# Experts' gate and up products in two halves, and scatters through views that do not overlap

## The chip, the cores and the metric

The kernel runs on one core of a Trainium2 chip. The time is the device time of one execution, in microseconds (us). The engines of the core run side by side and wait for each other through semaphores: TensorE (PE) multiplies and transposes, VectorE (DVE) and ScalarE (ACT) work element by element, GpSimd (POOL) does the same and issues the indirect scatters, and SyncE (SP) issues the ordinary DMAs.

## The reference

The input `x` has 8 sequences of 64 rows of 512 numbers, so 512 rows in all. Each context has 1601 rows of 512 numbers. All numbers are fp32. Three blocks follow one another, each added to `x`:

```
x = x + cross_attention(layernorm(x), ctx)       # one head of 512, softmax over 1601 rows
x = x + attention(layernorm(x))                  # 16 heads of 32, sigmoid instead of softmax
x = x + experts(layernorm(x))                    # 8 experts, each row goes to one
```

In the last block a row's expert is the largest of 8 gate products. The row, times the sigmoid of that largest product, goes through its expert: `g = xs @ w_gate.T`, `u = xs @ w_up.T` (512 to 256 each), then `(u * silu(g)) @ w_down.T` back to 512.

## The kernel before, in words

The 512 rows are four tiles of 128 (`i` or `p` from 0 to 3), two sequences each. A main loop over the tiles does the cross-attention of tile `p`, with the steps of the second block for tiles `p - 1` and `p - 2` between its products. Behind the loop stands an ending: the second block's steps for tiles 2 and 3, and the experts.

The steps are small functions with a name and a number, and `do(...)` calls them in the order in which they are written. PE's order is exactly this order, for a manual schedule is open on PE from the start; in the ending SP's order is written out too, and POOL's inside `routed`. The orders of DVE, ACT and, elsewhere, POOL are planned by the compiler from the dependences and its own costs. PE takes its instructions in order: one that waits holds up all behind it.

Steps of the second block for tile `i`, with the PE work that the trace shows for each:

- `turn`: four transposes of the normalized rows (`t_xh`), copied to `xhT` and `xvT` by DVE and ACT.
- `unit_q`, `unit_k`: a projection of four products, one for each chunk of 128 of the contraction (`p_q`, `p_k`; the trace counts two matmul instructions for each fp32 product), then a normalization by ACT and DVE.
- `gates`: POOL and DVE only. `values`: a projection (`p_v`), scaled by DVE.
- `split`: transposes of q and k (`t_q`, `t_k`). `align`: 64 small matmul instructions (`al`, L490), sigmoid by ACT into `res`.
- `sums`: 64 small matmul instructions (`co`, L508), scaled by DVE. `back`: transposes (`t_c`), copied by ACT into `cT`. `output`: a projection (`p_o`), added to `x` by DVE.
- `face`: transposes of the result (`t_x`). `gated`: the gate products (`pl`, L621, 8 columns wide) and a chain of tiny DVE instructions.
- `routed`: counts of rows for each expert (`pr`, `pf`), a slot for each row, and two indirect scatters by POOL into DRAM: the scaled rows into `xd` (L676), the rows with their index into `rd` (L699). A slot is a row of `xd` and `rd`; no two rows of `x` get the same.

Every row of `xd` belongs to one expert: parts of 32 rows, so that a tile of 128 slots holds 32 rows of each of four experts. Six such tiles (`k` from 0 to 5) are computed; even ones belong to experts 0 to 3, odd ones to experts 4 to 7. A later branch for the case that an expert gets more than 96 rows is not entered with these inputs. The steps of a tile:

- `fetch(part)`: SP loads tiles `2*part` and `2*part + 1` of `xd` and `rd` (L868). It waits for all scatters before it: `fetch(0)` stands behind those of `x` tiles 0 and 1, `fetch(1)` behind that of tile 2, `fetch(2)` behind that of tile 3.
- `flip(k)`: four transposes (`t_xe`), copied by ACT to `xeT`.
- `up(k)`: the gate and up products (`gu`, L879): for each of four chunks of the contraction, four experts side by side in the array, so 16 products, or 32 matmul instructions in the trace. Then ACT's sigmoid and two DVE products make `h`.
- `over(k)`: two transposes of `h` (`ht`, L893), copied by DVE to `hT`.
- `down(k)`: 8 products (`y`, L903, 16 instructions); DVE adds the rows of `rd` (L908), and POOL scatters the 128 rows into the result (L909). Slots that no row has taken carry an index that is out of bounds and are left out.

The ending of before, from the last steps of tile 2 on:

```
fetch(0)
do((turn, 2), (unit_q, 2), (at_turn, 3), (unit_k, 2), (at_out, 3), (norm, 3), (gates, 2))
do((values, 2), (split, 2), (turn, 3), (flip, 0), (up, 0), (align, 2), (unit_q, 3))
do((over, 0), (sums, 2), (unit_k, 3), (flip, 1), (back, 2), (down, 0), (gates, 3))
do((output, 2), (split, 3), (values, 3), (face, 2), (align, 3), (gated, 2), (sums, 3))
do((routed, 2))
```

PSUM has eight banks, which all products share (`bank`). The large row buffers are 22 of one size (`row`). Between instructions that touch the same DRAM tensor the framework sets a wait where it can't tell that their rows differ; the rows of an indirect scatter are known only at run time, so two scatters into one tensor wait for one another, by landing.

Of the kernel before, what the change touches and what calls it, by code (L numbers as in the profile page):

```python
# [8 lines left out]

# [10 lines left out]
NT = B * S // P  # L20
DC = D // P
# [4 lines left out]
PARTS = 3  # L26
# [9 lines left out]
def perceiver_kernel(ctx: ExitStack, tc: tile.TileContext, out: bass.AP, t: dict):  # L36
# [16 lines left out]
    def row(name):  # L53
        return rowp.tile([P, D], F32, tag="row", name=name)
# [4 lines left out]
    def bank(name):  # L59
        return banks.tile([P, D], F32, tag="bank", name=name)  # L60
# [4 lines left out]
    def tiny(n, tag, name):  # L65
        return small.tile([P, n], F32, tag=tag, name=name)
# [171 lines left out]
    with tc.manual_schedule(engines={mybir.EngineType.DVE, mybir.EngineType.Activation}):  # L238
# [19 lines left out]
        for i0 in (0, 2):  # L258
            cols = slice(i0 * P, (i0 + 2) * P)
            for ec in range(DC):  # L260
                ps = bank(f"qp{i0}_{ec}")
                for dc in range(DC):
                    nc.tensor.matmul(  # L263
                        ps[:, : 2 * P], lhsT=wq[:, dc, ec * P : (ec + 1) * P],
                        rhs=xnT[:, dc, cols], start=(dc == 0), stop=(dc == DC - 1),
# [265 lines left out]
    ffw = {}  # L531
# [10 lines left out]
    def load_experts():  # L542

        gu, dn = {}, {}
        gu[0] = load_gate_up(0, slab("wgu0"))
        gu[1] = load_gate_up(1, one.tile([P, DC, D], F32, tag="R", name="wgu1"))
        for e in range(2, E):
            if e - 2 < 5:
                dn[e - 2] = load_down(
                    e - 2, blkp.tile([P, IC, D], F32, tag="blk", name=f"wd{e - 2}")  # L550
                )
            gu[e] = load_gate_up(e, slab(f"wgu{e}"))
        return gu, dn
# [14 lines left out]
    xd = tc.dram_tile([E * ROWS, D], F32, name="xd")  # L568
    rd = tc.dram_tile([E * ROWS, D + 4], F32, name="rd")

    def blank_rows():
        blank = blkp.tile([P, D + 4], F32, tag="blk", name="blank")
        nc.gpsimd.memset(blank[:, :D], 0.0)
        nc.gpsimd.memset(blank[:, D:].bitcast(I32), 1 << 20)
        for r in range(0, E * CAP, P):
            nc.gpsimd.dma_start(out=xd[r : r + P, :], in_=blank[:, :D])
            nc.gpsimd.dma_start(out=rd[r : r + P, :], in_=blank)
# [63 lines left out]
    def route(i, mean, rs, begin):  # L641

        ps = bank(f"pr{i}")
        pr = ps[:, :E]
        if i > 0:
            nc.tensor.matmul(pr, lhsT=ones, rhs=runs[-1], start=True, stop=False)
        nc.tensor.matmul(pr, lhsT=before, rhs=oh[:, i, :], start=(i == 0), stop=True)
        if i > 0:
            nrun = const.tile([P, E], F32, tag=f"run{i}", name=f"run{i}")
            nc.gpsimd.tensor_tensor(nrun, runs[-1], oh[:, i, :], ALU.add)  # L650
            runs.append(nrun)
        else:
            runs.append(oh[:, i, :])
        at = tiny(E, "at", f"at{i}")
        nc.vector.tensor_tensor(at, pr, oh[:, i, :], ALU.mult)
        place = tiny(1, "place", f"place{i}")
        nc.vector.tensor_reduce(place, at, AX.X, ALU.add)
        slot_i = const.tile([P, 1], I32, tag=f"slot{i}", name=f"sloti{i}")
        if i < NT - 1:

            part = small.tile([P, 1], I32, tag="part", name=f"part{i}")
            nc.vector.tensor_copy(part, place)
            nc.vector.tensor_scalar(part, part, 0x7FE0, None, ALU.bitwise_and)
            at1 = tiny(1, "at1", f"at1_{i}")
            nc.vector.scalar_tensor_tensor(at1, part, E - 1.0, place, ALU.mult, ALU.add)
            nc.vector.tensor_scalar(slot_i, at1, begin, None, ALU.add)
        else:

            past = tiny(1, "at1", f"past{i}")
            nc.vector.tensor_scalar(past, place, CAP - 0.5, 4.0 * E * ROWS, ALU.is_ge, ALU.mult)  # L670
            nc.vector.scalar_tensor_tensor(slot_i, place, begin, past, ALU.add, ALU.add)
        by = tiny(1, "by", f"by{i}")
        nc.vector.tensor_tensor(by, rw[:, i : i + 1], rs, ALU.mult)
        xr = row(f"xr{i}")
        nc.vector.tensor_scalar(xr, xs[i], mean, by, ALU.subtract, ALU.mult)
        nc.gpsimd.indirect_dma_start(  # L676
            out=xd[:, :], out_offset=bass.IndirectOffsetOnAxis(ap=slot_i, axis=0),
            in_=xr, in_offset=None, bounds_check=E * ROWS - 1, oob_is_err=False,
        )
        return slot_i  # L680
# [16 lines left out]

    def send_rows(i, xb, slot_i):
        nc.gpsimd.indirect_dma_start(  # L699
            out=rd[:, :], out_offset=bass.IndirectOffsetOnAxis(ap=slot_i, axis=0),  # L700
            in_=xb, in_offset=None, bounds_check=E * ROWS - 1, oob_is_err=False,
        )

# [66 lines left out]
    def routed(i):  # L770
        xb = keep_rows(i)
        with tc.manual_schedule(engines={mybir.EngineType.Pool}):
            slot = route(i, *tile_of[i]["spread"])
            send_rows(i, xb, slot)
        if 0 < i < NT - 1:
            raised(i)
# [8 lines left out]
    def do(*steps):  # L785
        for f, i in steps:
            f(i)
# [15 lines left out]
    for p in range(NT):  # L803
        i = p - 2
# [27 lines left out]
        if p == 1:  # L832
            blank_rows()
# [21 lines left out]
    gu, dn = load_experts()  # L855
    NR = 2 * PARTS

    def columns(k):
        return [(4 * (k % 2) + j, slice(j * PART, (j + 1) * PART)) for j in range(4)]

    xes, xbs, xTs, hs = {}, {}, {}, {}

    def fetch(part):

        for src, dst in ((xd, xes), (rd, xbs)):
            for k in (2 * part, 2 * part + 1):
                dst[k] = rowp.tile([P, src.shape[-1]], F32, tag="row", name=f"in{k}_{src.shape[-1]}")
                nc.sync.dma_start(out=dst[k], in_=src[k * P : (k + 1) * P, :])  # L868
# [2 lines left out]
        xTs[k] = row4(f"xeT{k}")  # L871
        nc.scalar.copy(xTs[k], transposed(xes.pop(k), f"xe{k}"))  # L872

    def up(k):
        xT = xTs.pop(k)
        ps = bank(f"gu{k}")
        for dc in range(DC):
            for e, c in columns(k):
                nc.tensor.matmul(  # L879
                    ps[c, :], lhsT=xT[:, dc, c], rhs=ffw[e][0][:, dc, :],  # L880
                    start=(dc == 0), stop=(dc == DC - 1),
                )
        h = rowp.tile([P, FI], F32, tag="row", name=f"h{k}")
        nc.scalar.activation(h, ps[:, :FI], AF.Sigmoid)  # L884
        nc.vector.tensor_tensor(h, ps[:, :FI], h, ALU.mult)  # L885
        nc.vector.tensor_tensor(h, ps[:, FI:], h, ALU.mult)
        hs[k] = h
# [10 lines left out]
    def down(k):  # L898
        hT = hs.pop(k)
        y = bank(f"y{k}")  # L900
        for ic in range(IC):
            for e, c in columns(k):
                nc.tensor.matmul(  # L903
                    y[c, :], lhsT=hT[:, ic, c], rhs=ffw[e][1][:, ic, :],
                    start=(ic == 0), stop=(ic == IC - 1),
                )
        xb = xbs.pop(k)
        nc.vector.tensor_tensor(xb[:, :D], y, xb[:, :D], ALU.add)  # L908
        nc.gpsimd.indirect_dma_start(  # L909
            out=out[:, :],  # L910
            out_offset=bass.IndirectOffsetOnAxis(ap=xb[:, D : D + 1].bitcast(I32), axis=0),
            in_=xb[:, :D], in_offset=None, bounds_check=B * S - 1, oob_is_err=False,
        )
# [3 lines left out]
    fetch(0)  # L917
    load_experts_late(gu, dn)
    do((turn, 2), (unit_q, 2), (at_turn, 3), (unit_k, 2), (at_out, 3), (norm, 3), (gates, 2))
    do((values, 2), (split, 2), (turn, 3), (flip, 0), (up, 0), (align, 2), (unit_q, 3))  # L920
    do((over, 0), (sums, 2), (unit_k, 3), (flip, 1), (back, 2), (down, 0), (gates, 3))
    do((output, 2), (split, 3), (values, 3), (face, 2), (align, 3), (gated, 2), (sums, 3))
    do((routed, 2))
    fetch(1)
    do((up, 1), (back, 3), (over, 1), (output, 3), (down, 1), (face, 3), (flip, 2))
    do((gated, 3), (up, 2), (routed, 3))
    fetch(2)

    ps = bank("pc")
# [2 lines left out]
    nc.vector.tensor_reduce(most, ps[:, :E], AX.X, ALU.max)  # L932
    nc.vector.tensor_scalar(flag, most, CAP + 0.5, None, ALU.is_ge)

    do((over, 2), (flip, 3), (up, 3), (down, 2), (over, 3), (down, 3))
    do((flip, 4), (up, 4), (flip, 5), (over, 4), (up, 5), (down, 4), (over, 5), (down, 5))
    spill = nc.values_load(flag[0:1, 0:1], min_val=0, max_val=1)  # L937
    last.close()
    order.close()
# [3 lines left out]
    with tc.If(spill != 0), ExitStack() as ph:  # L943
# [16 lines left out]
        for e in range(E):  # L960
# [11 lines left out]
                wb, lhsT=ones, rhs=dg.rearrange("p i q -> p (i q)"), start=True, stop=True  # L972
# [6 lines left out]
            for ic in range(IC):  # L979
                pgu = []  # L980
                for k in range(2):
                    ps = ps_g.tile([P, B * S], F32, tag="gu", name=f"dgu{e}_{ic}_{k}")
                    for dc in range(DC):
                        c0 = k * FI + ic * P
                        nc.tensor.matmul(
                            ps, lhsT=wgu[:, dc, c0 : c0 + P], rhs=xsT[:, dc, :],
# [70 lines left out]
```

## Time and profile before

| what | value |
|---|---|
| three runs | 328.46, 331.7 and 332.65 us; median 331.7 |
| the profiled execution's own time | 333.91 us |
| its span, from the first to the last instruction | 332.2 us |
| mean granted TensorE clock | 0.95 |
| first instruction that the new order moves (`p_v` of tile 2 starts) | 232.38 us |
| last product (`y` of tile 5) ends | 324.26 us |
| last scatter is issued | 327.36 us |

The times of all views count from the start of the span. A group in the timeline has its start, its length, engine, line, operation, the tiles that it writes and reads, its shape and its count; in brackets stands how long the engine stood idle before it, and who released it. The windows view has for each stretch the busy time of PE, weight loads (PEld), DVE, ACT and POOL with their instructions, and then the granted clock, the DMA share and GB/s.

### The profile page before, as it was taken

How to read it: one execution, taken by the hardware profiler on the slowest of the kernel's cores; microseconds unless marked ns; L12 is line 12 of the kernel's file. 1: busy time of each engine (PE TensorE's matmuls, PEld its weight loads, DVE VectorE, ACT ScalarE, POOL GpSimd, SP SyncE). 2: the span in 40 equal slices, each digit the busy share in tenths (PEclk: the TensorE clock that was granted, in tenths of full speed). 3: DMA queues.
4: the chain of work that ended last, by engine and by line, in shares of the span. 5: the costliest groups of instructions: out<-in, count | busy, mean ns of one | idle time of the engine just before them, and what ended most of it. 6: DMA issues, size and time to landing. Idle time of an engine off the chain costs nothing. (4 is left out here: it accounts for less than half of the span.)

```text
span 332.2 us, 6425 instructions
## 1 busy us (share of the span) xinstructions
PE 298.7 (90%) x2652; PEld 157.5 (47%) x2652; DVE 161.9 (49%) x416; ACT 92.0 (28%) x192; POOL 60.7 (18%) x93
## 2 busy tenths in 40 slices
PE   5999699999999899998999999999699999889790
PEld 4776365643553245644434654434356464342220
DVE  5215477234751677655586845324614743452120
ACT  3133104330055020366331435314342240120100
POOL 4003630500161005001023000220400412031111
PEclk9799699999999999999999999999979985997996
DMA  8999800179893980000893028699601002305101
GB/s 275 426 418 310 346 6 2 37 275 417 316 353 110 386 325 6 4 0 8 314 372 132 2 84 299 224 310 357 248 2 65 29 2 67 125 28 174 54 7 35
DMA packets 19712, 57.71 MB, mean 174 GB/s; under 512 B 2210, under 2 KB 10450, under 8 KB 15712
## 3 DMA queue, kind: packets, MB, share of 16 engines
q1 hardware_dynamic: 16992, 50.37, 42.0%
q0 software_dynamic: 2400, 6.89, 5.6%
q8 instruction: 23, 0.38, 0.5%
q14 instruction: 9, 0.07, 0.1%
q10 hardware_dynamic: 288, 0.00, 0.0%
HBM read 50.94 MB, written 6.84 MB: 174 GB/s over the span
## 5 line engine op out<-in xcount | busy, mean ns | idle before, releaser
L221 DVE STREAM_TRANSPOSE T<-cx 128x512 f32<-128x512 f32 x96 | 61.8, 681 | 36.5 <-DMA cx<-in_ctx_dram 25.1
L326 PE MATMUL sc<-T,R 32*64 32x416 f32 (+2 forms) x1024 | 51.9, 524 | 2.8 <-DVE qb L291 2.7
L382 PE MATMUL ac<-cx,pt 128*64 128x512 f32 x192 | 43.8, 598 | 1.8 <-ACT pt L372 1.8
L326 PEld LDWEIGHTS sc<-T,R 32*64 32x64 f32 x1024 | 28.6, 138 | 21.8 <-issue 8.3
L879 PE MATMUL gu<-wgu,xeT 128*32 128x512 f32 x192 | 28.1, 732 | 4.8 <-ACT xeT L872 4.8
L382 PEld LDWEIGHTS ac<-cx,pt 128*64 128x64 f32 x192 | 12.7, 136 | 24.4 <-issue 21.2
L263 PE MATMUL qp<-xnT,w_xWq 128*128 128x256 f32 x64 | 15.9, 412 | 2.5 <-DMA w_xWq<-in_xWq_dram 1.7
L879 PEld LDWEIGHTS gu<-wgu,xeT 128*32 128x32 f32 x192 | 8.3, 130 | 19.8 <-issue 14.3
L457 POOL TENSOR_TENSOR gm_k<-qn_k,c_gk 128x512 f32<-128x512 f32 x4 | 5.1, 1272 | 67.2 <-DVE qn_k L452 67.2
L174 PE MATMUL p_q<-w_aWq,xhT 128*128 128x512 f32 x32 | 14.8, 605 | 2.5 <-DVE xhT L428 2.5
L885 DVE TENSOR_TENSOR h<-gu,h 128x256 f32<-128x256 f32 x6 | 2.5, 424 | 28.9 <-ACT h L884 28.9
L299 POOL COPY q<-qk 128x512 f32<-128x512 f32 x16 | 9.1, 615 | 40.8 <-ACT qk L284 40.8
L420 POOL TENSOR_TENSOR x<-x,c_bo 128x512 f32<-128x512 f32 x4 | 5.1, 1268 | 60.4 <-DVE xh L419 60.4
L263 PEld LDWEIGHTS qp<-xnT,w_xWq 128*128 128x128 f32 x64 | 13.1, 208 | 4.9 <-ACT rs_a L246 1.9
L174 PE MATMUL p_o<-w_aWo,cT 128*128 128x512 f32 x32 | 14.7, 602 | 0.7 <-ACT cT L524 0.7
L174 PE MATMUL p_po<-w_xWv,acT 128*128 128x512 f32 x32 | 14.5, 595 | 0.7 <-ACT acT L394 0.7
L174 PE MATMUL p_qk<-w_xWkT,qpT 128*128 128x512 f32 x32 | 14.7, 601 | 0.0
L174 PE MATMUL p_k<-w_aWk,xhT 128*128 128x512 f32 x32 | 14.5, 595 | 0.0
L174 PE MATMUL p_v<-w_aWv,xvT 128*128 128x512 f32 x32 | 14.4, 592 | 0.0
L372 ACT COPY pt<-pp 128x512 f32<-128x512 f32 (+1 forms) x16 | 7.8, 525 | 23.2 <-PE pp L370 23.1
L903 PE MATMUL y<-wd,hT 128*32 128x512 f32 x96 | 11.5, 596 | 1.6 <-DVE hT L895 1.6
L337 DVE TENSOR_REDUCE mx<-sc 128x1 f32<-128x416 f32 (+2 forms) x16 | 8.1, 567 | 9.3 <-PE sc L326 9.3
(187 smaller groups left out, 406.4 us busy)
## 6 DMA issues: line engine op xcount, KB each, us to landing
cx<-in_ctx_dram SPq DMA_DIRECT2D x24, 1024.0 KB, 10.4
wgu<-in_wgT_dram SPq DMA_DIRECT2D x8, 512.0 KB, 8.4
wgu<-in_wuT_dram SPq DMA_DIRECT2D x8, 512.0 KB, 7.0
wd<-in_wdT_dram SPq DMA_DIRECT2D x8, 512.0 KB, 8.6
rd<-blank POOLq DMA_DIRECT2D x6, 258.0 KB, 4.7
in<-rd SPq DMA_DIRECT2D x6, 258.0 KB, 4.3
xd<-blank POOLq DMA_DIRECT2D x6, 256.0 KB, 4.5
in<-xd SPq DMA_DIRECT2D x6, 256.0 KB, 5.0
```

What stands on the lines that cost most here:

```text
L174: nc.tensor.matmul(ps, lhsT=srcT[:, dc, :], rhs=w[:, dc, :], start=(dc == 0), stop=(dc == DC - 1),)
L221: nc.vector.transpose(T[:, :, 128 * g : 128 * g + 128].rearrange("p b (c k) -> p b c k", k=32), cxs[p, g][b2][:, :, 128 * q : 128 * q + 12 ...
L263: nc.tensor.matmul(ps[:, : 2 * P], lhsT=wq[:, dc, ec * P : (ec + 1) * P], rhs=xnT[:, dc, cols], start=(dc == 0), stop=(dc == DC - 1),)
L299: nc.gpsimd.tensor_copy(q4, qk[:, 32 * b0 : 32 * b0 + 128].rearrange("p (b d) -> p b d", d=32).unsqueeze(2).to_broadcast([P, 4, 4, 32]),)
L326: nc.tensor.matmul(sc[a][r : r + S, : WIDTH[a]], lhsT=R[32 * a : 32 * a + 32, b, r : r + S], rhs=Ts[b2][32 * a : 32 * a + 32, j, : WIDTH[a ...
L337: nc.vector.tensor_reduce(mx[:, a : a + 1], sc[a][:, : WIDTH[a]], AX.X, ALU.max)
L372: nc.scalar.copy(pt[:m, :nch, :], tp[:m, :nch, :])
L382: nc.tensor.matmul(ac[r : r + S, :], lhsT=pt[:m, j, r : r + S], rhs=rhs, start=(g == 0 and j == 0), stop=(g == 3),)
L420: nc.gpsimd.tensor_tensor(xs[i], xs[i], bo, ALU.add)
L457: nc.gpsimd.tensor_tensor(heads(gm), heads(qn), gb.unsqueeze(1).to_broadcast([P, H, HD]), ALU.mult)
L879: nc.tensor.matmul(ps[c, :], lhsT=xT[:, dc, c], rhs=ffw[e][0][:, dc, :], start=(dc == 0), stop=(dc == DC - 1),)
L903: nc.tensor.matmul(y[c, :], lhsT=hT[:, ic, c], rhs=ffw[e][1][:, ic, :], start=(ic == 0), stop=(ic == IC - 1),)
```

## The change

The step `up` is cut in two. `up_first` takes a bank and does the first two of the four chunks of the contraction (8 products, 16 instructions); `up_last` does the other two into the same bank, and then the sigmoid and the products as before. The order of the ending is written anew: other steps stand between the halves, `flip` 0 comes ahead of `values` 2, `down` 0 and `down` 1 come later, and in the last lines transposes and halves of different tiles alternate. The scatters into `xd`, `rd` and the result go through views of these tensors, one for each scatter. The framework takes the views of a tensor for disjoint, so that it sets no wait between scatters through two of them; a plain access to the tensor, like the loads of `fetch`, is still ordered against all of them.

```diff
+    xd_of = dram_disjoint_views(xd[:, :], NT)
+    rd_of = dram_disjoint_views(rd[:, :], NT)
+    out_of = dram_disjoint_views(out, 2 * PARTS)
...
-            out=xd[:, :], out_offset=bass.IndirectOffsetOnAxis(ap=slot_i, axis=0),
+            out=xd_of[i], out_offset=bass.IndirectOffsetOnAxis(ap=slot_i, axis=0),
...
-            out=rd[:, :], out_offset=bass.IndirectOffsetOnAxis(ap=slot_i, axis=0),
+            out=rd_of[i], out_offset=bass.IndirectOffsetOnAxis(ap=slot_i, axis=0),
...
-    def up(k):
-        xT = xTs.pop(k)
-        ps = bank(f"gu{k}")
-        for dc in range(DC):
+    def up_first(k):
+
+        ps = hs[k] = bank(f"gu{k}")
+        up_chunks(k, ps, range(DC // 2))
+
+    def up_chunks(k, ps, chunks):
+        for dc in chunks:
             for e, c in columns(k):
                 nc.tensor.matmul(
-                    ps[c, :], lhsT=xT[:, dc, c], rhs=ffw[e][0][:, dc, :],
+                    ps[c, :], lhsT=xTs[k][:, dc, c], rhs=ffw[e][0][:, dc, :],
                     start=(dc == 0), stop=(dc == DC - 1),
                 )
+
+    def up_last(k):
+        ps = hs[k]
+        up_chunks(k, ps, range(DC // 2, DC))
         h = rowp.tile([P, FI], F32, tag="row", name=f"h{k}")
...
-            out=out[:, :],
+            out=out_of[k],
...
-    do((values, 2), (split, 2), (turn, 3), (flip, 0), (up, 0), (align, 2), (unit_q, 3))
-    do((over, 0), (sums, 2), (unit_k, 3), (flip, 1), (back, 2), (down, 0), (gates, 3))
-    do((output, 2), (split, 3), (values, 3), (face, 2), (align, 3), (gated, 2), (sums, 3))
+    do((flip, 0), (values, 2), (split, 2), (up_first, 0), (turn, 3), (align, 2), (up_last, 0))
+    do((unit_q, 3), (over, 0), (sums, 2), (unit_k, 3), (back, 2), (flip, 1), (output, 2))
+    do((split, 3), (gates, 3), (face, 2), (values, 3), (gated, 2), (align, 3), (up_first, 1))
     do((routed, 2))
     fetch(1)
-    do((up, 1), (back, 3), (over, 1), (output, 3), (down, 1), (face, 3), (flip, 2))
-    do((gated, 3), (up, 2), (routed, 3))
+    do((sums, 3), (up_last, 1), (back, 3), (down, 0), (output, 3), (over, 1), (flip, 2))
+    do((flip, 3), (face, 3), (up_first, 2), (gated, 3), (up_last, 2), (routed, 3))
     fetch(2)
...
-    do((over, 2), (flip, 3), (up, 3), (down, 2), (over, 3), (down, 3))
-    do((flip, 4), (up, 4), (flip, 5), (over, 4), (up, 5), (down, 4), (over, 5), (down, 5))
+    do((up_first, 3), (over, 2), (up_last, 3), (down, 2), (over, 3), (down, 1), (flip, 4))
+    do((down, 3), (flip, 5), (up_first, 4), (up_last, 4), (up_first, 5), (over, 4))
+    do((up_last, 5), (down, 4), (over, 5), (down, 5))
```

## The prediction

> **What bounds it now.** I read the busy shares first, then the slices, then TensorE's (PE's) timeline over the last 100 us, and last GpSimd's (POOL's) timeline at the very end. The first lines are from the page.
>
> ```profile
> PE 298.7 (90%) x2652; PEld 157.5 (47%) x2652; DVE 161.9 (49%) x416; ACT 92.0 (28%) x192; POOL 60.7 (18%) x93
> ...
> PE   5999699999999899998999999999699999889790
> ...
> PEclk9799699999999999999999999999979985997996
> ```
>
> PE is busy 90% of the span; no other engine passes 49%. So the end is set by PE's own order of work, its stalls, and its clock: the clock row is full except near the start and in the last quarter (7, 8, 5, 7). The diff touches PE's order only behind the last `gates`, that is behind 232.38 us, where the value product of tile 2 starts. PE's timeline from there:
>
> ```profile
> 237.12 0.60 PE L168 MATMUL t_xe<-ident,in 128*128 128x128 f32 x4
> 241.12 5.39 PE L879 MATMUL gu<-wgu,xeT 128*32 128x512 f32 x32 [3.39 <-ACT xeT L872]
> ...
> 251.30 2.06 PE L508 MATMUL co<-vg,res 64*64 64x32 f32 x64
> ...
> 270.84 4.08 PE L508 MATMUL co<-vg,res 64*64 64x32 f32 x64 [0.51 <-ACT res L497]
> ...
> 276.23 6.45 PE L879 MATMUL gu<-wgu,xeT 128*32 128x512 f32 x32
> ...
> 292.26 3.64 PE L879 MATMUL gu<-wgu,xeT 128*32 128x512 f32 x32
> ...
> 298.87 5.34 PE L879 MATMUL gu<-wgu,xeT 128*32 128x512 f32 x32 [0.67 <-ACT xeT L872]
> ...
> 322.34 1.92 PE L903 MATMUL y<-wd,hT 128*32 128x512 f32 x16 [0.78 <-DVE hT L895]
> ```
>
> Columns: start, length, instructions, stall in brackets. The same 32 matmuls take 3.64 us or up to 6.45, and the same 64 `co` matmuls 2.06 or 4.08. The windows view says why (granted clock in the column behind POOL):
>
> ```profile
> 238.00:240.00 2.00, 0.00 (x0) 0.00 (x0) 1.08 (x3) 0.81 (x2) 0.00 (x0) 1.00 0.03 10
> ...
> 242.00:244.00 2.00, 2.00 (x15) 1.30 (x11) 0.00 (x0) 0.36 (x1) 0.00 (x0) 0.50 0.03 8
> ...
> 272.00:274.00 2.00, 2.00 (x40) 2.00 (x40) 0.16 (x1) 0.06 (x1) 0.19 (x1) 0.50 0.00 0
> ```
>
> The clock records give the half-rate stretches: 240.97 to 244.39, 271.69 to 281.94 and 299.00 to 302.42 us, multiples of 3.41. The first follows an idle stretch. The other two follow 3.4 us without a longer stall than 0.67, but filled with small products: `al`, `pl` and `co` before 271.69; `pr`, `pc` and transposes before 299.00.
>
> **The change, part by part.** Durations are from one start to the next at full clock: four transposes 0.44, a projection 3.43 to 3.53, `al` 1.02, `co` 1.99, `pl` 0.99, `pr`+`pf` 0.69, `ht` 0.31, `y` 1.84, half of the gate and up products 1.78 (292.26 to 295.83, halved).
>
> *Stalls that go*, from the brackets of PE's timeline: 3.39 (first products behind `xeT`; now a projection and two transposes, 4.3 us, stand between), 0.16 (`p_o`), 0.51 (`co` behind `res`; now 2.5 us between), 1.00 (`over` 1; now 5.8 between), 0.29 (`pl`; half a product between), 0.66 (`over` 2: the chain from products to `h` takes 1.43, 295.83 to 297.26, and the half product put between takes 1.78), 0.67 (`up` 3; its flip is now far ahead), 0.78 (`down` 3; now 2.3 between), 0.72 (`up` 4; now 2.3 between), 0.98 (`over` 4; half product). Sum 9.2. The 0.78 of the last `down` stays.
>
> *Clock that comes back*: gate and up products 0, 1 and 3: 5.39, 6.45 and 5.34 against 3.64, so 1.75 + 2.81 + 1.70; `co` 2.0; `pr`/`pf` 1.38 against 0.69. Sum 9.0, if no window turns small again. The worst place in the new order is between the halves of product 1: `pr`, `pf` and `co`, 2.7 us, with 1.78 of dense work on each side, and 2.0 of `pl` and `al` ahead. A 3.41 us window there can hold as little as 0.71 of dense work. The trace brackets the limit: 251.22 to 254.63 held 1.33 dense and 2.0 `co` and stayed at 1.00; 322.90 to 326.31 held 1.36 and idle time and fell. I take nothing for this place, up to 1.7 for one window.
>
> [...]
>
> *New stalls.* (1) `flip` 0 moves ahead of the value product, so PE is ready for it at 232.38, but its rows land only at 234.39 (last semaphore step of that load, issued at 225.39 to 227.56 into queues that run at a share of 1.0). PE takes work in order, so 2.0 us; behind it wait the value product, the split and everything later. Bounds 1.3 to 3.3, by the landings of its neighbours in the queue (233.69 and 235.72). The window 230.73 to 234.14 then holds 1.65 dense; I take no clock loss, up to 1.7. (2) `output` 2 has only a flip between itself and its `cT`: transposes 0.60 and copy 0.59 against 0.88, so 0.4. (3) `flip` 4 comes 8.5 us behind tile 3's `pr` instead of 13.1. The way of its rows: `pr` at 295.83, slots 297.78, scatter 298.06 to 302.74, fetch 302.87, landed 305.53: 9.7 us; with tile 2's scatter (278.18 to 280.92, 2.74 instead of 4.68) 7.8 us. So nothing to 1.2; I take 0.1, since five of the six result scatters also took 2.6 to 2.7. New stalls sum to 2.5.
>
> *The halving* adds no instruction: 32 matmuls remain, in 16 and 16. Six more changes of kind on PE cost 0 to 0.15 each; nothing taken. A `gu` bank is held longer by 1.5 to 2.7 us of other work; with four `al`, one `gu`, one `pl` and two of `pr`/`pf` that is all eight banks once, but `pl` and `al` are read (1.57 for four sigmoids) before `co` needs theirs: nothing, up to 1.6. ScalarE and VectorE get the same instructions; their order is planned anew: nothing taken, up to 2, by the largest waits of this stretch that two engines gave each other on short chains (1 to 2 us). SyncE keeps its order; `down` 1 later holds a row buffer longer.
>
> *Views.* Before, each scatter into a tensor waits for the previous one's landing. For `xd` and `rd` that had landed 50 us earlier (225.18 against 278.18) or 17 (280.92 against 298.06): nothing. The last result rows do wait:
>
> ```profile
> 322.23 0.97 POOL L909 DMA_INDIRECT out_dram<-in  x1 [10.94 <-DVE in L908]
> 327.36 0.98 POOL L909 DMA_INDIRECT out_dram<-in  x1 [4.16 <-issue]
> ```
>
> The sum for the last scatter is ready at 325.05 (324.36 + 0.69), the one before lands at 326.60, and POOL issues at 327.36. Elsewhere POOL starts 0.28 behind the sum (306.68 to 306.96), so 325.33: 2.0 us go. Had the earlier scatter landed in 2.6 like most, only 0.2 would go. Below nothing: scatters that overlap landed in 4.1 to 4.7 (`xd` and `rd` of tile 3), which would cost 1.5 at most. I take 2.0, the row itself.
>
> **The sum**: 9.2 + 9.0 - 2.5 = 15.7 on PE, 2.0 at the end: 17.7 off the profiled execution's own 333.91 (its span is 332.2), 316.2. That execution lies 2.2 above the median shown, 331.7; a median run that already lacks part of the clock loss would come out at the same place, one that lacks it elsewhere at 314. Forecast 316.
>
> **Rivals.**
> *A. Clock losses stay in part.* If the small products still pull a window or two down, each costs 1.7 (half of 3.41), and a stretch like 271.69 to 281.94 costs 5.5: 318 to 322. For it: the 2.7 us between halves; the 2.0 us wait at `flip` 0. Against: 251.22 to 254.63. If the drops follow nothing in PE's order but the one idle stretch, only 1.75 of the 9.0 comes back: 323.5. [...]
>
> *B. The lateness moves.* ScalarE's and VectorE's planned orders put `h` or `xeT` behind other work, PE waits at each second half or `over`. Six places at 1 to 2 us, plus A's 5.5, eat 11.5 to 17.5: 328 to 334. For it: the brackets show PE waiting for just these two engines. Against: they are busy 28% and 49%, and each new gap is longer than the chain it covers.
>
> *C. Slower.* The dense work is cut to 1.78 us pieces, and PE's clock never settles: 275.10 to 278.51 held 2.3 us of gate and up products and stayed at 0.50. From 234 to 306 us there are 21 windows of 3.41; each at half rate costs 1.7, so 10 undo the gain and 13 make it over 2% slower (338.3 and more). For it: that window. Against: dense work at half rate lasts twice as long and so fills its window, as 278.51 to 281.94 did.
>
> [...]
>
> *D. The views do nothing* because something else holds POOL's last issue (the row says "issue"): 318.
>
> **Chances.** Forecast with D, 312 to 319: 0.62. A: 0.18 (of it 0.08 for 323.5). B: 0.12. C: 0.08. Two per cent of the median, 6.6 us, is about what a measurement of this kernel can tell from no change (its runs spread over 4.2), so faster needs under 325.1. Faster 0.80, same 0.12, slower 0.08. The range goes from 312 (all of the unknowns at their good end, seen from the median: 331.7 - 19.7) to 325, which takes in A and leaves B and C, 0.20, out.
>
> **What would show it.** In the changed profile: all 32 matmuls of a `gu` in two groups of about 1.8 us; the clock at 1.00 from 235 to the last product; a stall of 2 us at the first `t_xe`, released by the load of rows; none over 0.5 behind `hT`, `xeT` or `h` before the last `down`; the last `y` ending at 307 to 310; two last scatters about 3 us apart, the second 0.3 behind its sum. The forecast is wrong if half-rate stretches beyond one window appear behind 235, if the first `t_xe` waits over 4 us, or if `t_xe` 4 waits over 2.

## The result, and the profile after

| | before | after |
|---|---|---|
| median of four runs | 331.67 us | 316.99 us |
| runs | 328.46 to 332.65 | 313.56 to 318.70 |
| ratio to before | | 0.95, 95% interval 0.9379 to 0.9621 |
| profiled execution, its span | 333.91, 332.2 | 315.56, 313.8 |
| mean granted clock | 0.95 | 0.988 |

The change makes the kernel 5% faster; the forecast was 316. Of the four runs after, 318.41 and 318.70 count as slow, because they lie over 1.5% above the fastest, and the ratios in this document are of the fast runs alone; the two medians give 0.956. The page of the changed kernel has these rows for what was shown of before (busy shares, PE and its granted clock in forty slices):

```profile
PE 289.0 (92%) x2652; PEld 151.6 (48%) x2652; DVE 161.9 (52%) x416; ACT 91.9 (29%) x192; POOL 61.0 (19%) x93
...
PE   5899699999999989999899999999979989999992
...
PEclk9799899999999999999999999999999999999999
```

The instructions on PE are the same 2652, and they are busy for 9.7 us less, because none of them behind 40 us runs at half rate (some 1.7 us of it lie ahead of 43 us, where before had a longer half-rate stretch): the 7, 8, 5 and 7 of the last quarter are gone. PE's timeline shows what is left of the stalls:

```profile
232.22 0.66 PE L169 MATMUL t_xe<-ident,in 128*128 128x128 f32 x4 [1.61 <-DMA in<-xd]
...
237.11 1.92 PE L888 MATMUL gu<-wgu,xeT 128*32 128x512 f32 x16
...
254.67 3.70 PE L175 MATMUL p_o<-w_aWo,cT 128*128 128x512 f32 x8 [1.52 <-ACT cT L525]
...
267.66 2.06 PE L509 MATMUL co<-vg,res 64*64 64x32 f32 x64
...
306.04 1.92 PE L916 MATMUL y<-wd,hT 128*32 128x512 f32 x16 [0.77 <-DVE hT L908]
```

These three brackets are the only ones behind 232 us; an idle time under 0.15 us gets none. A half of the gate and up products takes 1.92 us, and `co` of tile 3, which took 4.08, takes 2.06. At the end, POOL's timeline has the last two scatters 3.1 us apart instead of 5.1:

```profile
305.94 0.98 POOL L922 DMA_INDIRECT out_dram<-in  x1 [8.84 <-DVE in L921]
309.03 0.97 POOL L922 DMA_INDIRECT out_dram<-in  x1 [2.12 <-DVEq L957]
```

To compare executions without the early part, which the new order doesn't touch and whose half-rate stretches differ from run to run, I cut each profiled span at two starts: that of `p_po` of tile 3 (228.95 in before), the last product that all these kernels start with, and that of the last `y` (322.34).

| kernel | `p_po` to last `y` | half rate in it | last `y` to span end |
|---|---|---|---|
| before | 93.39 | 17.1 | 9.8 |
| after | 79.03 | 0 | 7.8 |

The difference of the spans, 18.3 us before rounding, is 14.4 in the stretch that was reordered, 2.0 behind the last `y`, and 1.9 ahead of `p_po`. The last part is not the change's, as far as the profiles tell: there before ran 6.83 us at half rate from 36.17 on, after 3.41 from 36.37 on, which is 1.7.

### The profile page after: what moved, and what is told of

Its sections match the earlier page's. It is cut to its first block, busy times and chain, and to the rows that moved or that the text cites. A ratio compares the mean times of both kernels' runs of the same rounds, so it can differ in the third digit from the quotient of the medians.

```text
span 313.8 us, 6416 instructions
## 1 busy us (share of the span) xinstructions
PE 289.0 (92%) x2652; PEld 151.6 (48%) x2652; DVE 161.9 (52%) x416; ACT 91.9 (29%) x192; POOL 61.0 (19%) x93
## 5 line engine op out<-in xcount | busy, mean ns | idle before, releaser
L327 PE MATMUL sc<-T,R 32*64 32x416 f32 (+2 forms) x1024 | 50.4, 512 | 2.6 <-DVE qb L292 2.3
L327 PEld LDWEIGHTS sc<-T,R 32*64 32x64 f32 x1024 | 27.8, 135 | 21.0 <-issue 8.0
L888 PE MATMUL gu<-wgu,xeT 128*32 128x512 f32 x192 | 22.7, 597 | 0.0
L175 PE MATMUL p_qk<-w_xWkT,qpT 128*128 128x512 f32 x32 | 14.7, 601 | 0.0
L175 PE MATMUL p_v<-w_aWv,xvT 128*128 128x512 f32 x32 | 14.4, 592 | 0.0
L228 DVE STREAM_TRANSPOSE T<-tail 96x128 f32<-96x128 f32 x32 | 8.5, 271 | 3.9 <-DMA tail<-in_ctx_dram 3.9
L175 PEld LDWEIGHTS p_o<-w_aWo,cT 128*128 128x128 f32 x32 | 5.8, 189 | 9.4 <-issue 6.6
```

Of the source, the lines that this page charges most:

```text
L175: nc.tensor.matmul(ps, lhsT=srcT[:, dc, :], rhs=w[:, dc, :], start=(dc == 0), stop=(dc == DC - 1),)
L228: nc.vector.transpose(T[:96, :, 384:416], cxs[p, 3][b2][:, 128 * q : 128 * q + 128].rearrange("p (b d) -> p b d", d=32),)
L327: nc.tensor.matmul(sc[a][r : r + S, : WIDTH[a]], lhsT=R[32 * a : 32 * a + 32, b, r : r + S], rhs=Ts[b2][32 * a : 32 * a + 32, j, : WIDTH[a ...
L888: nc.tensor.matmul(ps[c, :], lhsT=xTs[k][:, dc, c], rhs=ffw[e][0][:, dc, :], start=(dc == 0), stop=(dc == DC - 1),)
```

## The experiments

The theory under test: the gain is the sum of (a) stalls that other steps now cover, (b) clock that PE keeps, because dense halves stand between runs of small products, and (c) the wait for the previous scatter at the end. Rivals: the clock falls only when PE is idle; the halving does nothing and the order all; the views do more than shorten the end. All numbers are from the profiled executions, by the two cuts above, and ratios are to the kernel before, run on the same chip.

| kernel | `p_po` to last `y` | half rate in it | last `y` to span end | ratio, interval |
|---|---|---|---|---|
| no_views | 79.12 | 0 | 10.3 | 0.9623, 0.9541 to 0.9704 |
| views_only | 91.50 | 13.7 | 7.8 | 0.9932, 0.9892 to 0.9972 |
| small_filler | 88.39 | 10.2 | 7.8 | 0.9775, 0.9692 to 0.9859 |
| dense_filler | 83.15 | 0 | 7.9 | 0.9713, 0.9609 to 0.9816 |
| whole_early | 86.09 | 6.8 | 7.8 | 0.9760, 0.9689 to 0.9831 |
| whole_late | 86.84 | 6.8 | 7.9 | 0.9764, 0.9689 to 0.9839 |
| flip_behind_values | 76.74 | 0 | 7.8 | 0.9476, 0.9417 to 0.9535 |
| both_stalls_out | 75.33 | 0 | 7.8 | 0.9411, 0.9340 to 0.9481 |

### The views: off, and alone

The changed kernel without the views:

```diff
-            out=xd_of[i], out_offset=bass.IndirectOffsetOnAxis(ap=slot_i, axis=0),
+            out=xd[:, :], out_offset=bass.IndirectOffsetOnAxis(ap=slot_i, axis=0),
...
-            out=rd_of[i], out_offset=bass.IndirectOffsetOnAxis(ap=slot_i, axis=0),
+            out=rd[:, :], out_offset=bass.IndirectOffsetOnAxis(ap=slot_i, axis=0),
...
-            out=out_of[k],
+            out=out[:, :],
```

> The changed kernel with plain accesses to xd, rd and the result in place of the views; the order of the steps is the changed one. Theory (the views matter at the last scatter alone): POOL's last issue waits again for the landing of the scatter before it, so it comes 0.7 to 0.8 us behind that landing instead of 0.3 behind its sum (in the changed kernel's profile the earlier scatter landed at 310.51 and the last was issued at 309.03): 2.2 us more than the changed kernel if that landing takes 3.6 to 4.6 us, 0.2 if it takes 2.6. TensorE's last product ends where it does in the changed kernel, 308, within 2. Rival (the views also set the earlier scatters and fetches free): stalls at the flips of tiles 2 to 5, and the last product ends over 2 us later.

PE's part is the changed kernel's within 0.1 us (79.12 against 79.03), and the end is 2.5 us longer. (The ratios, 0.9623 and 0.95, lie 4 us apart, but their intervals overlap.) POOL's timeline of this kernel, its last four scatters:

```profile
297.09 0.98 POOL L918 DMA_INDIRECT out_dram<-in  x1 [4.24 <-DMA out_dram<-in]
300.54 0.98 POOL L918 DMA_INDIRECT out_dram<-in  x1 [2.47 <-DMA out_dram<-in]
306.35 0.98 POOL L918 DMA_INDIRECT out_dram<-in  x1 [4.83 <-DVE in L917]
311.96 0.98 POOL L918 DMA_INDIRECT out_dram<-in  x1 [4.63 <-issue]
```

The first two wait for the landing of their predecessor too, by name, but nobody waits for them. The last is issued 0.76 us behind the landing before it (311.20) and 2.5 us later than in the changed kernel, counted from the last `y` (306.46 to 311.96 against 306.04 to 309.03). The rival expected PE to end later; it doesn't.

The other way round, the views went into the kernel before and its order stayed.

> The kernel before with the views alone, its order untouched. Theory: 0.2 to 2.0 us less than before (329.7 to 331.5), all of it between the last sum on VectorE and the last scatter's issue, which comes 0.3 us behind the sum; the half-rate stretches and the stalls of TensorE stay. Rival (the order would not be enough without the views, part of the gain is theirs): 5 us less or more.

The end shrinks from 9.8 to 7.8 us, as expected. The ratio 0.9932 of a median of 330.24 is 2.2 us (the medians differ by 3.2), just above the expected 0.2 to 2.0 and below the rival's 5. The stalls stand where they stood (PE's timeline has the same ten brackets ahead of the last `y`), and two of the three half-rate stretches lie over the same products as before, but with other lengths: 236.60 to 243.43, 6.83 us instead of 3.42, and 270.73 to 277.56, 6.83 instead of 10.25. The third is missing, without anything in the order there having changed; I come back to that.

### What pulls the clock down: filler, small and dense

Between the sums of tile 3 and the second half of product 1 stand extra products whose result nobody reads. They have no dependence that could make PE wait.

```diff
-    do((sums, 3), (up_last, 1), (back, 3), ...
+    sums(3)
+    idle_products(18, ident[:, :8])              # small; dense: idle_products(5, ffw[0][0][:, 0, :])
+    do((up_last, 1), (back, 3), ...
```

> The changed kernel with 18 extra products of 8 columns (36 instructions, by the gate products' rate of 0.124 us each some 4.5 us) between the 64 small products of tile 3's sums and the second half of product 1; their result is not used. The run of small work there grows from 2.7 to 7.2 us, without an idle gap. Theory (TensorE's clock falls when a window of 3.41 us holds mostly small products, idle or not): the granted clock falls to 0.50 behind 269 for one to three windows; 4.5 us of work plus 1.7 to 5 of lost clock, so 6 to 10 us more than the changed kernel, 321.5 to 325.5 where that has 315.6. Rival (only idle time pulls the clock down): it stays at 1.00, 4.5 us more, 320.

> The same place, with 5 extra products of 512 columns (10 instructions at 0.43 us, 4.3 us) instead of the small ones; their result is not used. Both theories: 4.3 us more than the changed kernel, 319.9, and the granted clock at 1.00 throughout. If the clock falls here too, the kind of product is not what decides.

The windows view of the kernel with the small filler, cut at the clock's own boundaries; PE's busy time stands behind the length, the granted clock behind POOL:

```profile
265.60:268.96 3.36, 3.36 (x65) 1.93 (x52) 1.66 (x9) 3.04 (x6) 0.85 (x3) 1.00 0.02 5
268.96:272.38 3.42, 3.42 (x76) 3.38 (x72) 2.06 (x7) 0.00 (x0) 2.01 (x2) 1.00 0.22 78
272.38:275.80 3.42, 3.42 (x18) 3.42 (x17) 0.00 (x0) 0.00 (x0) 0.00 (x0) 0.50 0.48 144
275.80:279.20 3.40, 3.40 (x18) 1.58 (x21) 0.00 (x0) 0.00 (x0) 0.00 (x0) 0.50 0.74 246
279.20:282.62 3.42, 3.42 (x20) 1.12 (x16) 0.85 (x2) 0.97 (x2) 0.00 (x0) 0.50 0.00 0
282.62:286.00 3.38, 3.38 (x17) 1.18 (x10) 0.69 (x1) 0.00 (x0) 0.98 (x1) 1.00 0.00 0
```

PE's busy time fills 268.96 to 272.38, with `co` and filler alone, and at the end of that window the clock halves, from 1.00 to 0.50. So no idle time that the profile shows was needed in this run; the rival falls in that form. A short pause inside the small products is not excluded: the filler's products start 0.11 us apart and are each counted as busy for 0.26, with modelled ends, so the row can't tell whether the array works all that time. It comes back only behind 279.20 to 282.62: the window ahead of that held 2.4 us of gate and up products (they start at 276.80), and the clock stayed at 0.50 behind it. The cost is 9.36 us on PE's path: half of 10.24, 5.1, is clock, and 4.0 is the filler itself (6.19 us from 270.61 to 276.80, of which 4.42 at half rate); the first flip also waited 0.4 longer in this execution (2.02 against 1.61). The dense filler, from PE's timeline:

```profile
265.58 2.06 PE L509 MATMUL co<-vg,res 64*64 64x32 f32 x64
267.57 4.56 PE L116 MATMUL idle<-wgu,ident 128*128 128x512 f32 x10
272.06 1.92 PE L888 MATMUL gu<-wgu,xeT 128*32 128x512 f32 x16
```

It adds 4.12 us, 4.3 were expected, and the clock stays at 1.00 from 14 us to behind the last product. PE's busy time is full in both: 3.42 of 3.42 us with filler of 8 columns, and 0.50 behind it; 4.40 of 4.40 us (267.60 to 272.00) with filler of 512 columns, and 1.00 there and behind it. What differs is the kind of product. One execution of each kernel was profiled; the medians, 322.99 with the small filler and 319.61 with the dense one, go the same way.

### The halves: undivided at one place or the other

In one kernel `up_first` does all 32 matmuls and `up_last` nothing, in the other the reverse. The order of all steps is the changed one.

```diff
     def up_first(k):
         ps = hs[k] = bank(f"gu{k}")
-        up_chunks(k, ps, range(DC // 2))
+        up_chunks(k, ps, range(DC))
+        finish(k, ps)                     # sigmoid and products
     def up_last(k):
-        ...
+        pass                              # in the other kernel: up_first passes, up_last does range(DC)
```

> The changed order, but each gate and up product undivided at the place of its first half. Theory (the second halves cover chains, and they break up runs of small products): new stalls behind the sums of tile 3 (the scaling of 1.45 us, then the transposes, before dense work comes again) and before tile 3's counts (gate chain, 1.1 us), 2.5 us together; the small run behind tile 2's counts grows from 2.7 to some 4.5 us, and the clock may fall for one window there, 1.7 us. 2.5 to 6 us more than the changed kernel: 318 to 321.5. Rival (the new order does it all, the halving nothing): same as the changed kernel within 1 us.

> The changed order, but each gate and up product undivided at the place of its second half. Theory: gate products, alignment, counts and sums of tiles 2 and 3 stand in one run of 4.7 us with a stall for ScalarE's sigmoids (some 2 us) in it, so that the clock falls there for one to three windows (1.7 to 5 us); further stalls before tile 3's gate products (1.3) and before the second transposes of products 2 and 4 (0.7 to 1 each). 6 to 10 us more than the changed kernel: 321.5 to 325.5. Rival (halving does nothing): same as the changed kernel within 1 us.

Both lose about half of what the change won: 7.06 and 7.81 us on PE's path, and 2.6 points of the ratio. (Their intervals reach to 0.983 and 0.984, so it is not certain that they beat before by 2%.) The rival, that halving does nothing, falls. PE's timeline of the early one shows both kinds of loss:

```profile
268.98 2.06 PE L509 MATMUL co<-vg,res 64*64 64x32 f32 x64
272.53 0.92 PE L169 MATMUL t_c<-ident,cg 128*128 128x128 f32 x4 [1.50 <-DVE cg L518]
273.39 3.29 PE L918 MATMUL y<-wd,hT 128*32 128x512 f32 x16
...
287.85 0.39 PE L653 MATMUL pr<-oh,before 128*128 128x8 f32 x2 [1.23 <-DVE begin L644]
...
288.73 5.34 PE L889 MATMUL gu<-wgu,xeT 128*32 128x512 f32 x32
```

Without a second half behind `co`, PE waits 1.50 us for VectorE's scaling; `co` and the wait fill the window 269.37 to 272.78, and behind it the clock is at 0.50 until 276.19 (`y` 3.29 instead of 1.92). The same happens at tile 3's counts, which I had not foreseen (289.85 to 293.26; the `gu` there takes 5.34 instead of 3.64). Stalls beyond the changed kernel's sum to 4.0 (1.50, 1.23, 0.18 and twice 0.52), the clock to 3.4. Together that is 7.4, which accounts for the 7.06; the expected 2.5 to 6 was too low by the second window and the two 0.52. In the late one, stalls sum to 4.4 and one stretch of 6.83 us at half rate (266.3 to 273.1, 0.50) costs 3.4, within the expected 6 to 10. Its timeline around the sums of tile 3, and two of the stalls that come back behind them:

```profile
264.97 0.30 PE L509 MATMUL co<-vg,res 64*64 64x32 f32 x4 [0.65 <-ACT res L498]
265.51 3.68 PE L509 MATMUL co<-vg,res 64*64 64x32 f32 x60 [0.24 <-ACT res L498]
269.12 5.61 PE L887 MATMUL gu<-wgu,xeT 128*32 128x512 f32 x32
...
283.11 1.06 PE L627 MATMUL pl<-gwc,x3T 128*128 128x8 f32 x8 [0.78 <-ACT x3T L762]
...
305.34 0.41 PE L905 MATMUL ht<-ident,h 128*128 128x128 f32 x2 [1.56 <-DVE h L898]
```

### The two stalls that the change added

First the flip of tile 0 goes behind the value product, and tile 3's turn ahead of the first half:

```diff
-    do((flip, 0), (values, 2), (split, 2), (up_first, 0), (turn, 3), (align, 2), (up_last, 0))
+    do((values, 2), (flip, 0), (split, 2), (turn, 3), (up_first, 0), (align, 2), (up_last, 0))
```

> The changed kernel with the flip of tile 0 behind tile 2's value product, and tile 3's turn ahead of the first half of product 0. Theory (the 1.6 us stall at the first flip is the landing of its rows, and nothing else is late there): it goes, 1.6 us less than the changed kernel, and the first half of product 0 waits for nothing over 0.3. Rival (the time comes back at the next wait, for tile 3's turned rows): less than 0.5 us gained.

The stall is gone without a new one, and PE's path is 2.29 us shorter, 0.7 more than expected. 0.3 of that stood between `p_q` of tile 3 and the transposes of `h` behind it, whose starts were 3.83 apart (242.42 to 246.25) and are now 3.54 (240.81 to 244.35). The eight instructions of `p_q` keep the same distances in both. But in the changed kernel `h` was ready only at 246.10, because its sigmoid on ScalarE stood behind a table load and the four sigmoids of `res` (242.06 to 244.92); now it is ready at 243.12, 1.2 us before PE wants it. PE's idle time there was 0.13 us, too short for a bracket. The other 0.4 lie in the distances between groups at changes of kind.

Then also the copy of tile 2's sums moves ahead of the square roots of tile 3's keys, and the first down product is halved:

```diff
-    do((unit_q, 3), (over, 0), (sums, 2), (unit_k, 3), (back, 2), (flip, 1), (output, 2))
+    do((unit_q, 3), (over, 0), (sums, 2), (k_head, 3), (back, 2), (k_tail, 3), (flip, 1),
+       (down_a, 0), (output, 2))
...
-    do((sums, 3), (up_last, 1), (back, 3), (down, 0), (output, 3), ...
+    do((sums, 3), (up_last, 1), (back, 3), (down_b, 0), (output, 3), ...
```

`k_head` is the projection and the squares of `unit_k`, `k_tail` the rest; `down_a` and `down_b` are 8 instructions of the trace each, one chunk of the contraction.

> The same, and besides ScalarE's copy of tile 2's sums placed ahead of the square roots of tile 3's keys (it stood behind them, and those waited 0.96 us for VectorE), and the 16 matmuls of the first down product in two halves, one ahead of each output projection. Theory: the 1.5 us stall before tile 2's output projection goes too, so 3.1 us less than the changed kernel in all; TensorE's last product ends at 304.9 where the early part is like the changed kernel's. Rival (the square roots come later and hold up tile 3's keys, whose transposes stand right behind the projection): 1.6 us in all, like the kernel with the flip alone.

ScalarE's timeline of the changed kernel, where the stall came from:

```profile
252.37 0.60 ACT L446 ACTIVATE sq_k<-p_k 128x512 f32<-128x512 f32 x1 [4.09 <-PE p_k L175]
253.93 0.22 ACT L450 ACTIVATE ss_k<-ss_k 128x16 f32<-128x16 f32 x1 [0.96 <-DVE ss_k L449]
254.05 0.57 ACT L525 COPY cT<-t_c 128x512 f32<-128x512 f32 x1
```

and of the new one:

```profile
247.57 0.60 ACT L448 ACTIVATE sq_k<-p_k 128x512 f32<-128x512 f32 x1 [3.77 <-PE p_k L175]
248.06 0.58 ACT L530 COPY cT<-t_c 128x512 f32<-128x512 f32 x1
249.13 0.22 ACT L455 ACTIVATE ss_k<-ss_k 128x16 f32<-128x16 f32 x1 [0.48 <-DVE ss_k L454]
```

ScalarE takes its list in order too: the copy, ready at 252.7, started at 254.05, behind square roots that waited 0.96 us for VectorE. In the new kernel it comes directly behind the squares, and `p_o` starts without a bracket. PE's path is 3.70 us shorter than the changed kernel's (3.1 expected), its only bracket is the last one, 0.77, and the median is 310.53 us against 330.36 of before; the ratio is 0.9411 (0.9340 to 0.9481). This is the fastest version measured. The last two edits were made together, so the runs do not say which of them would have been enough.

## Why the prediction was right, step by step

**What bounds the kernel**: PE, its stalls and its clock, as read. Stalls and clock left the span, and the busy time of the other engines is unchanged (DVE 161.9 us in both).

**Stalls that go, 9.2**: all ten brackets are gone, each behind the work that was named. Besides those that the prediction shows, PE's timeline of before had these, among others:

```profile
284.26 0.41 PE L893 MATMUL ht<-ident,h 128*128 128x128 f32 x2 [1.00 <-DVE h L886]
...
297.32 0.44 PE L893 MATMUL ht<-ident,h 128*128 128x128 f32 x2 [0.66 <-DVE h L886]
...
310.30 3.64 PE L879 MATMUL gu<-wgu,xeT 128*32 128x512 f32 x32 [0.72 <-ACT xeT L872]
...
315.50 0.41 PE L893 MATMUL ht<-ident,h 128*128 128x128 f32 x2 [0.98 <-DVE h L886]
```

That the halves are the cover is shown by the late undivided kernel, where three stalls come back at places for which the prediction names a half or a step between halves: 0.65 and 0.24 at `res`, 0.78 at `x3T`, 1.56 at `h`. The 1.50 and 1.23 of the early one are stalls that before did not have; there the new order needs the half.

**Clock that comes back, 9.0**: in the profiled run all of it (17.1 us at half rate, and none after). But half of 17.1 is 8.5, so about 0.5 of the 9.0 was not clock. It is in `co` of tile 3, which the prediction put down to the clock with 2.0: its first twelve instructions started in fours 0.36 us apart (270.84, 271.21, 271.57), the next at 271.94, each 0.05 us behind the end of one of ScalarE's four sigmoids of `res`. That was a wait, which no bracket shows, and the new order removed it too; so the sum stands, and its parts are a little off. The small filler showed again what the prediction read from two stretches of before: 268.96 to 272.38 held small products alone, without idle time in the profile, and the clock was at 0.50 behind it. As a number this term is not a constant. It belongs to one execution of before; the kernel with the views alone has 13.7 us at half rate in the same stretch and the same order. The likely reason, an estimate from the clock records, is where the windows of 3.41 us fall: in before and after every stretch between two changes of the granted clock lasts a whole multiple of 3.413 us (in before 3.41, 6.83 and 10.24 at 0.50, and among others 17.07, 23.89, 27.31 and 197.97 at 1.00), and the same work can lie differently in them. In before, the window ahead of the third half-rate stretch, 295.59 to 299.00, held 2.08 us of busy PE, 0.44 of it gate and up products; the corresponding one with the views, 291.21 to 294.62, held 2.62 and 0.98, and the clock stayed. A limit can't be read from this: in the early undivided kernel, 286.44 to 289.85 held 2.00 and 1.12, and the clock fell.

The sum of 17.7 was made against an execution of 333.91. Its counterpart is 18.3 shorter, of which 1.9 belong to the early part; the change itself brought 16.4 there, 1.3 less than the sum, and the medians differ by 14.7. That the median of 316.99 lies 1 us from the forecast is therefore in part luck: the two executions that were profiled, and the early part, came out that way. The lower end of the range, 331.7 - 19.7, is not added up in the prediction; the good ends that it states (1.3 at the first flip, nothing at `flip` 4) make 18.5, or 313.

**New stalls, 2.5**: 3.1 by the brackets. The wait at the first flip is 1.61 (2.0 forecast, 1.3 to 3.3 bounded). The one behind `cT` was mis-sized: 0.4 forecast, 1.52 measured. The forecast took transposes and copy as one chain and left out what ScalarE's planned order put between them, the square roots and their wait, 1.1 us. The wait at `flip` 4 did not come: its rows landed at 292.00, and PE was ready at 292.57.

**Halving and banks at nothing**: changes of kind cost 0.1 each where they can be seen (a half starts 0.53 behind `t_k` instead of 0.44), and no bracket names one of the eight banks of the kernel's pool (`bufs=8`). The sum on PE, 9.2 + 9.0 - 3.1 = 15.1, stands against 14.4 measured; those changes of kind and the 0.3 ahead of the transposes of `h` are what I can point to in the rest.

**Views, 2.0**: 2.0 measured, and 2.5 and 2.0 in the two kernels that isolate it. Rival D is out. The doubt that the earlier scatter might usually land in 2.6 us and leave 0.2 was unfounded: see below.

**Rivals**: of A, nothing in the profiled run. The four runs spread from 313.56 to 318.70, with mean clocks of 0.995 to 0.977; over a span of some 314 us that is 3 to 15 us at half rate anywhere, against 7.8 in the profiled one, all of it early or behind the last product. So some executions may lose a window or two more, but only one was profiled, and whether the 2.7 us between the halves is the place stays open. The part of A by which only the one idle stretch pulls the clock down, and which had 323.5 us, is excluded: the clock came back whole, and in the small filler it fell without idle time in the profile. B came true at `cT` for 1.1 us and at `over` 0 for 0.3, instead of at six places. C has its reason confirmed, for in the small filler a window with 2.4 us of dense work did not lift the clock from 0.50, but its cause never arose: with halves between the small products the clock stayed at 1.00 from 39.8 to 312.8 us.

## What to carry to other kernels

Where PE is the bound, look at the granted clock beside the stalls: in the small filler 3.42 us of 8- and 32-column products, without idle time on PE in the profile, had a clock of 0.50 behind them, and half of the gate and up products took 3.64 us instead of 1.92. One cure, the one tested here, is to cut a dense product and put its halves between the small ones: with the products undivided, at either place, 6.8 us of the reordered stretch ran at half rate, with the halves none. The same halves cover the chains on the other engines (in the late undivided kernel stalls of 4.4 us came back), but each engine's planned order has to be read along: here a copy that PE needed stood behind an instruction that waited 0.96 us, and PE waited 1.52. And where the last transfers go into one tensor, look whether the last one waits for the landing of the one before: here that cost 2.0 and 2.5 us.

## What the runs showed of the hardware

- Busy does not mean fast: by the profile PE was busy for 3.42 of 3.42 us in the window 268.96 to 272.38 of the small filler, and the clock halved behind it: it was at 0.50 from 272.38 to 282.62, and PE's timeline has no bracket from 262 to 290 us.
- The fifth result scatter was slow every time: in all ten profiled kernels it took 4.37 to 4.93 us from issue to landing, and the sixth, of the same size, 2.58 to 2.60. In the packets of before, after and the kernel without views a 16 KB instruction load starts at about the time the fifth scatter's packets do (after: 307.64 and 307.49; before: 324.30 and 323.78) and takes 1.0 to 1.8 us on one DMA engine. That this load is the reason is a guess; no run moved it, and the first two scatters of the changed kernel took 4.5 us as well.
